# Tiles of 32 channels by 4 states in the scan stage of a graph kernel

## The chip, the cores and the metric

The kernel runs on one core of a Trainium2 chip. The metric is the time of the whole launch in microseconds of the device. Engines: PE is TensorE's matmuls, PEld its weight loads, DVE is VectorE, ACT is ScalarE, POOL is GpSimd, SP issues most of the DMAs. Each engine takes its instructions in the order in which they are queued.

## The reference

Two layers, each a graph convolution and then a mixture of experts, on 4096 rows of 256. The change lies in the first convolution of the first layer, which ends in a state-space scan:

```python
h = relu(adj @ x @ gcn_w + gcn_b)             # then a layer norm over the 256 features
xz = h @ w_in                                 # 512 channels xc, 512 channels z
u = silu(causal_conv4(xc) + conv_b)
dbc = u @ w_xp                                # 16 for dt, 16 for B, 16 for C
dt = softplus(dbc[:, :16] @ w_dt + b_dt)
dA  = exp(dt[:, :, None] * A[None])           # A = -exp(A_log), 512 channels x 16 states
dBu = dt[:, :, None] * B[:, None, :] * u[:, :, None]
def step(hst, inp):                           # over the 4096 rows
    dAt, dBut, Ct = inp
    hst = dAt * hst + dBut
    return (hst, hst @ Ct)                    # sum over the 16 states
y = (ys + u * D_skip) * silu(z);  x = x + y @ w_out
```

Everything is float32. The second half of the layers (routing, experts, top-k graph) is outside the change.

## The kernel before, in words

The scan stage goes over 8 chunks of 512 rows (`CW`), each in 32 steps (`STEPS`). Channels lie on partitions, 128 to a block (4 blocks, `MB`), rows along the free dimension. One step handles one channel block and two of the 16 states: 128 x 2 x 512 elements, in order of halves (two blocks), pairs of states (`g`), block in the half (`mi`).

- `inputs` (L1353): for each pair of states SP loads two rows of B (`bb`) and of C (`cb`) onto all partitions, 512 KB each. POOL multiplies `du = dt*u` with `bb` into `db` (L1363, two buffers).
- `decay` (L1368): ACT computes exp(dt*A) of one state into a bank of PSUM (`da`, three banks in turn).
- `scan` (L1384): one DVE scan per state over 512 rows, in place in `db`, starting from `state`.
- `product` (L1391): ACT copies the last column to `state`; DVE multiplies `db` with `cb` into `hc` (L1396, six buffers).
- `pair` (L1398): a DMA of POOL's queue adds the second half of `hc` onto the first.
- `total` (L1404): PE adds `hc` into `psy` with a 128 x 128 identity, one matmul of 512 columns a step; the first adds `u * D_skip` with a diagonal matrix. In the last chunk, from step 8 on, two matmuls take the place of the pair DMA.
- `gate` (L1418): DVE multiplies a finished block of `psy` with silu(z), a step after its last total.

Beside the scan of chunk c runs the front of chunk c+1, and the graph product of chunk c+2. The order of PE, DVE, ACT and POOL is written out by hand: `Front.PLAN` and `Front.EARLY` list by step what the front does (steps from 32 on fall into the chunk's own scan), in the loop at L1512. EARLY pieces stand between the scans and the product, PLAN pieces after the totals. `propagation` (L854) is the graph product: 64 pieces of two matmuls a chunk with tiles `at` of the adjacency matrix, 512 KB each, three buffers, four pieces to a tile. A planner (L1430 to 1441) puts the pieces into steps by costs of PE and DVE (`PE_STEP`, `DVE_STEP`, `PE_COST`, `DVE_COST`). SP's DMAs are queued by the framework's scheduler. `dt` and `du` of a whole chunk (`abs`, `exp`, `plus`, `log` on ACT, four `soft` operations on DVE, each for both halves) are finished before the chunk's first step, in SBUF. A total for step n-4 is emitted at step n. `Tail` and `Norm` blocks (output product, next norm) run in the last two chunks; `Last` closes the stage.

## Time and profile before

| | us |
|---|---|
| median of 3 runs | 2307.77 (2306.41 to 2309.53) |
| the profiled execution, its time | 2304.35 |
| its span, first to last instruction | 2302.6 |
| first scan to last scan of the stage | 159.4 to 1248 |
| a steady chunk of 32 steps | 136.5 |
| granted TensorE clock, mean | 0.951 |

The lines shown from here on are of this one execution. A line of the timeline gives the start, the time from the first start to the last end, engine, line, operation, tile written and tiles read, shape, count, and in brackets how long the engine had been idle and for what. A matmul in float32 shows as two passes, each with a weight load; its ends are modelled, so a busy PE may still have room. "issue" is idle time for which the profile shows no cause.

### The profile page before, as it was taken

What the parts mean: (1) busy time and instruction counts of PE and PEld (TensorE: products, weight loads), DVE (VectorE), ACT (ScalarE), POOL (GpSimd) and SP (SyncE); (2) the same over time, 40 slices, a digit from 0 to 9 for tenths busy, and PEclk for the clock granted to TensorE, in tenths of its full rate; (3) what the DMA queues carried; (4) which work ended last, traced back from release to release, by engine and by line L of the source; (5) the groups of instructions that cost most, each with busy time, mean ns of one, the idle gap of its engine ahead of it and who ended that gap; (6) DMA issues with size and microseconds to landing.
All of it is one profiled execution on the core that took longest, in us unless ns stands there. A gap on an engine that the chain in (4) does not pass through costs nothing. (4 is left out here: it accounts for less than half of the span.)

```text
span 2302.6 us, 28211 instructions
## 1 busy us (share of the span) xinstructions
PE 2103.2 (91%) x8291; PEld 1504.2 (65%) x8291; DVE 1801.3 (78%) x3193; ACT 1211.5 (53%) x2080; POOL 1395.4 (61%) x1057
## 2 busy tenths in 40 slices
PE   7899999999999999999799699996899989899994
PEld 6665565666646566555466588784588778678773
DVE  6949999999999999999998889314448999954342
ACT  4145746566575556657675232322488778533221
POOL 1028778777877877687764444442067777856652
PEclk9999999999999999999899799998899999999997
DMA  8549999998999999899885899863365555477794
GB/s 293 174 143 261 235 271 251 255 265 220 280 245 272 245 242 281 217 288 269 232 280 171 279 325 357 255 214 122 105 195 178 176 164 174 138 232 221 250 316 154
DMA packets 302678, 532.30 MB, mean 231 GB/s; under 512 B 31323, under 2 KB 170575, under 8 KB 301616
## 3 DMA queue, kind: packets, MB, share of 16 engines
q1 hardware_dynamic: 244720, 416.84, 55.7%
q0 software_dynamic: 57792, 113.54, 22.1%
q8 instruction: 69, 1.13, 0.2%
q14 instruction: 97, 0.79, 0.1%
HBM read 434.34 MB, written 49.02 MB: 210 GB/s over the span
## 5 line engine op out<-in xcount | busy, mean ns | idle before, releaser
L1363 POOL TENSOR_TENSOR db<-du,bb 128x1024 f32<-128x1024 f32 x256 | 607.7, 2374 | 322.0 <-ACT state L1392 72.0
L1386 DVE TENSOR_TENSOR_SCAN db<-da,state,db 128x512 f32<-128x512 f32 x512 | 627.3, 1266 | 23.9 <-ACT da L1379 21.4
L871 PE MATMUL pt<-at,gn 128*128 128x256 f32 x2048 | 487.4, 392 | 30.6 <-ACT pts L877 15.2
L871 PEld LDWEIGHTS pt<-at,gn 128*128 128x128 f32 x2048 | 401.7, 197 | 151.5 <-issue 63.2
L1379 ACT ACTIVATE da<-dt,negA 128x512 f32<-128x512 f32 x512 | 345.5, 688 | 236.4 <-DVE db L1386 226.3
L1396 DVE TENSOR_TENSOR hc<-db,cb 128x1024 f32<-128x1024 f32 x256 | 328.3, 1283 | 17.8 <-issue 0.4
L1875 PE MATMUL pf<-gn,f 128*128 128x256 f32 x1280 | 290.8, 388 | 0.0
L1413 PE MATMUL psy<-hc,ident 128*128 128x512 f32 x560 | 287.2, 606 | 0.0
L1875 PEld LDWEIGHTS pf<-gn,f 128*128 128x128 f32 x1280 | 248.3, 195 | 37.6 <-issue 3.3
L712 PE MATMUL ps_h<-xkT,wk 128*128 128x256 f32 x864 | 214.1, 390 | 13.3 <-DVE xkT L737 9.7
L697 PE MATMUL ps_y<-wk,hk 128*128 128x256 f32 x864 | 214.5, 383 | 0.2
L702 DVE TENSOR_TENSOR yk<-ps_y,bk 128x512 f32<-128x512 f32 x73 | 50.2, 687 | 204.6 <-PE ps_y L697 187.6
L1400 POOL DMA_DIRECT2D hc<-hc x232 | 202.5, 873 | 0.2
L712 PEld LDWEIGHTS ps_h<-xkT,wk 128*128 128x128 f32 x864 | 159.8, 194 | 49.3 <-DVE xkT L737 14.9
L1737 POOL DMA_INDIRECT x<-gnd,ls_idx x128 | 149.6, 1169 | 59.5 <-DMA gnd<-gn 20.1
L697 PEld LDWEIGHTS ps_y<-wk,hk 128*128 128x128 f32 x864 | 161.8, 192 | 21.7 <-ACT hk L716 1.4
L1413 PEld LDWEIGHTS psy<-hc,ident 128*128 128x128 f32 x560 | 105.5, 195 | 79.5 <-issue 56.5
L1737 POOL DMA_INDIRECT ring<-gnd,ls_idx x88 | 109.5, 1245 | 31.3 <-DVE x L1753 11.8
L1006 PE MATMUL ps_xz<-hT,w_in 128*128 128x512 f32 x256 | 116.5, 598 | 5.6 <-ACT zs L1019 4.1
L716 ACT ACTIVATE hk<-ps_h,d0r_b 128x256 f32<-128x256 f32 x104 | 48.9, 473 | 136.1 <-PE ps_h L712 136.1
L1023 PE MATMUL ps_xz<-xc,dK 128*128 128x512 f32 x256 | 114.8, 592 | 0.0
L1857 ACT ACTIVATE f<-at 128x1024 f32<-128x1024 f32 x80 | 84.4, 1055 | 50.1 <-PE pf L1875 41.1
(403 smaller groups left out, 3024.2 us busy)
## 6 DMA issues: line engine op xcount, KB each, us to landing
at<-in_adjT_dram SPq DMA_DIRECT2D x208, 512.0 KB, 5.0
bb<-bcd SPq DMA_DIRECT2D x128, 512.0 KB, 5.4
cb<-bcd SPq DMA_DIRECT2D x128, 512.0 KB, 5.2
hc<-hc POOLq DMA_DIRECT2D x232, 256.0 KB, 4.7
wk<-in_L_ffn_W_dram SPq DMA_DIRECT2D x70, 512.0 KB, 6.2
wk<-in_L_ffn_expert_w_dram SPq DMA_DIRECT2D x114, 256.0 KB, 4.2
ls_at<-in_adj_dram SPq DMA_DIRECT2D x32, 512.0 KB, 8.5
hc<-in_adj_dram SPq DMA_DIRECT2D x16, 512.0 KB, 4.7
```

The costliest lines, as they stand in the source:

```text
L697: nc.tensor.matmul(ps[:, j, :], hT[:, m, j * P:(j + 1) * P], w[:, m, :], start=(m == 0), stop=(m == kb_out - 1),)
L712: nc.tensor.matmul(ps[:, j, :], w[:, d, m * P:(m + 1) * P], xT[:, d, :], start=(d == 0), stop=(d == DB - 1),)
L871: nc.tensor.matmul(pt[:, k, :], xl[:, j, k * P:(k + 1) * P], at[:, jj, :], start=(j == 0 and k == 0), stop=(j == NT - 1 and k == DB - 1),)
L1006: nc.tensor.matmul(ps, w_in[:, k, m * P:(m + 1) * P], self.hT[:, k, :], start=(k == 0), stop=(k == DB - 1),)
L1363: nc.gpsimd.tensor_tensor(self.db, self.f.du[self.half][:, self.mi:self.mi + 1, :].to_broadcast([P, 2, CW]), self.bb, ALU.mult,)
L1379: nc.scalar.activation(da, self.f.dt[self.half][:, self.mi, :], AF.Exp, scale=negA[:, self.m, n:n + 1])
L1386: nc.vector.tensor_tensor_scan(self.db[:, j, :], da, self.db[:, j, :], state[:, self.m, n:n + 1], ALU.mult, ALU.add,)
L1396: nc.vector.tensor_tensor(self.hc, self.db, self.cb, ALU.mult)
L1400: nc.gpsimd.dma_start(self.hc[:, 0, :], self.hc[:, 1, :], accum_op=ALU.add)
L1413: nc.tensor.matmul(f.psy[m], ident, self.hc[:, j, :], start=False, stop=(self.g == GS - 1 and j == last),)
L1737: nc.gpsimd.indirect_dma_start(out=to[:, :], out_offset=None, in_=gnd[:, :], in_offset=bass.IndirectOffsetOnAxis(ap=lists.idx[:, q, s:s + ...
L1875: nc.tensor.matmul(pf[:, t, :], f[:, jj, t * P:(t + 1) * P], gn[:, j, :], start=(j == 0 and t % 2 == 0), stop=(j == NT - 1 and t % 2 == 1),)
```

## The change

A tile now holds 32 channels by 4 groups of states on its 128 partitions: partition 32r + k is channel k of the 32, with states 4r to 4r+3. A step takes 32 channels (`q`, four to a block) and two of the four states of each group (`p`, `j`), still 128 x 2 x 512 elements and 32 steps a chunk.

- `dt` and `du` are written to DRAM by halves of the channels (`dtd`, 1 MB) and read back spread over the four groups (`spread`, `dtu`, 512 KB, five buffers, emitted five steps ahead). B and C come four times a chunk (`states`). `soft` work is split by halves of the channels; the second half of it runs in steps 29 to 32.
- One scan goes over both halves of a step, 1024 elements. The first decay of the second half stays 0, so that the scan starts anew there; what is carried from the chunk before is added to that element beforehand by ACT (`join`, with exp(dt*A) of the first row from `carried`). Two `da` tiles of two banks each take the place of three banks; decays are emitted two steps ahead.
- The product with C stands one step behind the scan, `db` has three buffers, and `inputs` of step n+2 follow the product of step n-1.
- `total` takes two steps at a time, at least six steps back (`LAG`): for each half of the rows and each of the two steps, one matmul with `pick` (128 x 32, sums the four groups) writes the 32 partitions of `psy` that belong to `q`. `psy` has one buffer.
- The plan, the fill before the first step, the start of the front (`BEGIN`) and the closing of the stage move accordingly; `dp.place` and the last norm use `da`'s banks.

```diff
-        ps_y = s1.enter_context(tc.tile_pool(name="ps_y", bufs=2, space=PSUM, reuse_waits="tile"))
+        ps_y = s1.enter_context(tc.tile_pool(name="ps_y", bufs=1, space=PSUM, reuse_waits="tile"))
...
-        STEPS = H * 2 * GS
+        G4 = P // 32
+        STEPS = MB * G4 * (NS // 4) // 2
+        BEGIN = 3
+        LAG = 6
-        FILL = {11: 8, 12: 2, 14: 1, 17: 3, 19: 1, 22: 3, 23: 1, 24: 2, 25: 3, 26: 40}
...
-        PIECE, PE_STEP, DVE_STEP = 1.0, 1.1, 4.3
...
+        FILL = {6: 8, 7: 2, 9: 1, 12: 3, 14: 1, 17: 3, 18: 1, 19: 2, 20: 3, 21: 40}
+        FILLED = {7: 1, 8: 2}
+        PIECE, PE_STEP, DVE_STEP = 1.0, (1.8, 0.1), 4.25
+        PE_COST = {"gcn": 2.5, "turn": 0.8, "xz": 2, "conv": 4, "project": 2, "dt": 1}
+        DVE_COST = {"stats": 1.4, "soft": 1.45}
-        banks = ["d0", "d1", "d2"]
+        da = [ps_a.tile([P, 2, CW], F32, name=f"da{k}", tag=f"d{k}") for k in range(2)]
...
+                3: ["gcn 0", "gcn 1"], 4: ["biased 0", "biased 1"], 6: ["normal"],
+                7: ["fill 7", "turn 0", "turn 1"],
+                8: ["turned 0", "turned 1", "fill 8", "xz 0", "xz 1"], 9: ["in 0", "in 1"],
+                10: ["conv 0"], 11: ["conv 1"], 12: ["silu 0"], 13: ["xz 2", "xz 3"],
+                14: ["in 2", "in 3"], 15: ["conv 2"], 16: ["conv 3"], 17: ["silu 1"],
+                18: ["project 0", "project 1"], 19: ["scatter", "dt 0", "dt 1"],
+                20: ["abs 0", "abs 1", "exp 0"], 21: ["plus 0"], 22: ["log 0"],
+                25: ["dt 2", "dt 3"], 27: ["abs 2", "abs 3", "exp 1"], 28: ["plus 1"],
+                29: ["log 1"],
+                37: ["xz 4", "xz 5"], 38: ["in 4", "in 5", "xz 6", "xz 7"],
+                39: ["in 6", "in 7"], 44: ["silu 2"],
...
+                5: ["stats 0", "stats 1", "root"],
+                22: ["soft 0 0"], 23: ["soft 0 1"], 24: ["soft 0 2"], 25: ["soft 0 3"],
+                29: ["soft 1 0"], 30: ["soft 1 1"], 31: ["soft 1 2"], 32: ["soft 1 3"],
...
+                self.dtd, self.dtu, self.bc = {}, {}, {}
...
             def do_abs(self, m):
                 ps = self.ps.pop(("dt", m))
+                b = m % H
+                if b == 0:
+                    self.sp = w1p.tile([P, H, 2, CW], F32, name="sp", tag="tmp")
+                    self.t1 = w1p.tile([P, H, CW], F32, name="t1", tag="h")
+                    self.dt, self.du = self.sp[:, :, 0, :], self.sp[:, :, 1, :]
+                nc.scalar.activation(self.du[:, b, :], ps, AF.Abs, bias=b_dt[:, m:m + 1])
+                nc.scalar.activation(self.dt[:, b, :], ps, AF.Relu, bias=b_dt[:, m:m + 1])
+            def do_exp(self, a):
+                nc.scalar.activation(self.du, self.du, AF.Exp, scale=-1.0)
+            def do_plus(self, a):
+                nc.scalar.activation(self.t1, self.du, AF.Identity, bias=1.0)
+                nc.scalar.activation(self.t1, self.t1, AF.Identity, bias=minus1[:, :1])
+            def do_log(self, a):
+                nc.scalar.activation(self.du, self.du, AF.Ln, bias=1.0)
+            def do_soft(self, a, i):
+                t1, dt, du = self.t1, self.dt, self.du
...
+                    nc.vector.tensor_tensor(
+                        du, dt, self.us[:, a * H:a * H + H, :], ALU.mult
+                    )
+                    self.dtd[a] = dram.tile([P, H, 2, CW], F32, name=f"dtd{self.c}_{a}")
+                    nc.sync.dma_start(self.dtd[a], self.sp)
+                    fronts[self.c] = self
+            def spread(self, g):
+                m, q = divmod(g, G4)
                 a, b = divmod(m, H)
...
+                rows = self.dtd[a][32 * q:32 * q + 32, b]
+                t = self.dtu[g] = w2p.tile([P, 2, CW], F32, name="dtu", bufs=5)
+                nc.sync.dma_start(
+                    t, bass.AP(rows.tensor, rows.offset, [(0, G4)] + list(rows.ap))
+                )
+            def states(self, k, p):
+                r0 = NS * (k == "c") + 2 * p
+                rows = self.bcd[r0:r0 + 2, :]
+                t = self.bc[k, p] = w2p.tile([P, 2, CW], F32, name=f"{k}b{p}", bufs=1)
+                nc.sync.dma_start(
+                    t, bass.AP(rows.tensor, rows.offset,
+                               [(NS // G4 * CW, G4), (0, 32)] + list(rows.ap))
+                )
...
-                self.db = w2p.tile([P, 2, CW], F32, name="db")
+            def __init__(self, n):
+                self.n = n
+                self.c, self.i = divmod(n, STEPS)
+                self.m, r = divmod(self.i, 2 * G4)
+                self.p, self.q = divmod(r, G4)
+                self.g = G4 * self.m + self.q
+                self.f = fronts[self.c]
+                self.dtu = self.f.dtu[self.g]
+                self.paired = self.c < NC - 1 or self.i < 8
+            def inputs(self):
+                self.db = w2p.tile([P, 2, CW], F32, name="db", bufs=3)
                 nc.gpsimd.tensor_tensor(
...
+                    self.db, self.dtu[:, 1:2, :].to_broadcast([P, 2, CW]),
+                    self.f.bc["b", self.p], ALU.mult,
+                )
+            def carried(self):
+                return e0[:, self.m % 2, self.q, :]
+            def decays(self):
+                m, q, p = self.m, self.q, self.p
+                if self.c > 0 and p == 0:
+                    nc.scalar.activation(
+                        self.carried(), negA[:, q, m, 1::2], AF.Exp, scale=self.dtu[:, 0, 0:1]
+                    )
+                for j in range(2):
+                    s_ = 2 * p + j
+                    nc.scalar.activation(
+                        da[self.n % 2][:, j, j:], self.dtu[:, 0, j:], AF.Exp,
+                        scale=negA[:, q, m, s_:s_ + 1],
+                    )
+            def join(self):
+                if self.c > 0:
+                    first = self.db[:, 1, 0:1]
+                    nc.scalar.activation(
+                        first, state[:, self.g, 2 * self.p + 1:2 * self.p + 2], AF.Identity,
+                        scale=self.carried()[:, self.p:self.p + 1], bias=first,
+                    )
+            def scan(self):
+                flat = self.db.rearrange("p a t -> p (a t)")
                 nc.vector.tensor_tensor_scan(
...
+                    flat, da[self.n % 2].rearrange("p a t -> p (a t)"), flat,
+                    state[:, self.g, 2 * self.p:2 * self.p + 1], ALU.mult, ALU.add,
+                )
+            def keep(self):
+                if self.c < NC - 1:
+                    nc.scalar.copy(
+                        state[:, self.g, 2 * self.p:2 * self.p + 2], self.db[:, :, CW - 1]
+                    )
             def product(self):
...
                 self.hc = w2p.tile([P, 2, CW], F32, name="hc", bufs=6)
...
+                nc.vector.tensor_tensor(self.hc, self.db, self.f.bc["c", self.p], ALU.mult)
...
+            def total(self, other):
                 f, m = self.f, self.m
...
+                if self.p == 0 and self.q == 0:
+                    f.psy = ps_y.tile([P, CW], F32, name="psy", tag="psy")
+                    nc.tensor.matmul(f.psy, dD[:, m, :], f.us[:, m, :], start=True, stop=False)
                 last = 0 if self.paired else 1
                 for j in range(last + 1):
...
+                    for w in range(2):
+                        for st in (self, other):
+                            r, t = slice(32 * st.q, 32 * st.q + 32), slice(w * HW, w * HW + HW)
+                            nc.tensor.matmul(
+                                f.psy[r, t], pick, st.hc[:, j, t], start=False,
+                                stop=(self.p == 1 and j == last and w == 1),
+                            )
+                return self.p == 1 and other.q == G4 - 1
             def gate(self):
...
+                u = self.f.us[:, self.m, :]
+                nc.vector.tensor_tensor(u, self.f.psy, self.f.zs[:, self.m, :], ALU.mult)
...
-            negA = load(wp, a["L0_gnn_A_log"], "negA")
+            negA = wp.tile([P, G4, MB, NS // G4], F32, name="negA")
+            for r in range(G4):
+                for q in range(G4):
+                    nc.sync.dma_start(
+                        negA[32 * r:32 * r + 32, q],
+                        a["L0_gnn_A_log"][32 * q:32 * q + 32, :, 4 * r:4 * r + 4],
+                    )
...
-            state = wp.tile([P, MB, NS], F32, name="state")
+            state = wp.tile([P, MB * G4, NS // G4], F32, name="state")
+            e0 = wp.tile([P, 2, G4, 2], F32, name="e0")
+            pick = wp.tile([P, 32], F32, name="pick")
+            for r in range(G4):
+                sq = slice(32 * r, 32 * r + 32)
+                nc.scalar.copy(pick[sq, :], ident[sq, sq])
+            for k in range(2):
+                nc.vector.memset(da[k][:, 1, 0:1], 0.0)
...
-            for i in range(9, STEPS):
+            for i in range(4, 27):
...
+                if i == 6:
+                if i == 19:
+                    for p in range(2):
+                        fr.states("b", p)
+                        fr.states("c", p)
+                if i == 25:
+                    for g in range(G4):
+                        fr.spread(g)
...
+            ALL = NC * STEPS
+            for n in range(2):
+                steps.append(Step(n))
+                steps[n].inputs()
+                steps[n].decays()
+            fr = None
+            for n in range(ALL):
...
+                cur = steps[n]
+                if i == 6 and c > 0:
...
+                live = [(fronts[c], STEPS + i)] if n > 0 else []
+                if c == 0 and i < 6:
+                    live.insert(0, (fronts[0], 27 + i))
+                if i >= BEGIN and fr is not None:
+                    live.append((fr, i))
+                if n + 5 < ALL:
+                    c5, i5 = divmod(n + 5, STEPS)
+                    if i5 % (2 * G4) < G4:
+                        fronts[c5].spread(i5 // (2 * G4) * G4 + i5 % G4)
+                if fr is not None:
+                    if i == 27:
+                        fr.states("b", 0)
+                    elif i == 29:
+                        fr.states("c", 0)
+                    elif i == 30:
+                        fr.states("b", 1)
+                if i == 1 and c > 0:
+                    fronts[c].states("c", 1)
+                cur.scan()
+                cur.keep()
+                if n + 1 < ALL:
+                    steps[n + 1].join()
+                if n + 2 < ALL:
+                    steps.append(Step(n + 2))
+                    steps[n + 2].decays()
+                for f, k in live:
+                    f.at(k, Front.EARLY)
...
+                if n > 0:
+                    steps[n - 1].product()
+                if n + 2 < ALL:
+                    steps[n + 2].inputs()
                 if n > 0:
                     steps[n - 1].pair()
...
+                for st in gated:
+                    st.gate()
                 gated = []
...
+                if summed <= n - LAG or (summed <= n - 3 and not steps[summed].paired):
+                    if steps[summed].total(steps[summed + 1]):
+                        gated.append(steps[summed])
+                    summed += 2
+                for f, k in live:
+                    f.at(k)
...
+            steps[-1].product()
+            last.first(1)
+            for m in range(H, MB - 1):
+                last.add(1, m)
+            last.residual(1)
+            while summed < ALL:
+                for st in gated:
+                    st.gate()
+                gated = []
+                if steps[summed].total(steps[summed + 1]):
+                    gated.append(steps[summed])
+                summed += 2
+            for st in gated:
+                st.gate()
+            for hh in range(2):
+                last.add(hh, MB - 1)
```

## The prediction

> **What bounds the kernel now.** I read the engine totals, the busy times by stage, and then the timeline of the scan stage engine by engine. First the totals and one steady stretch (columns: stretch, length, then busy time and count of PE, PEld, DVE, ACT, POOL, the granted clock, DMA share, GB/s):
>
> ```profile
> PE 2103.2 (91%) x8291; PEld 1504.2 (65%) x8291; DVE 1801.3 (78%) x3193; ACT 1211.5 (53%) x2080; POOL 1395.4 (61%) x1057
> ...
> 560.00:700.00 140.00, 136.79 (x458) 86.26 (x457) 134.11 (x122) 84.57 (x147) 104.54 (x66) 0.98 0.94 255
> ```
>
> Both PE and DVE are nearly full there. The chunks' first scans start at 159.4, 294.7, 431.3, 567.8, 704.3, 840.9, 977.4 and 1117.3 us: a steady chunk of 32 steps takes 136.5 us. The timeline tells which engine paces one plain step:
>
> ```profile
> 703.19 1.23 DVE L1396 TENSOR_TENSOR hc<-db,cb 128x1024 f32<-128x1024 f32 x1
> ...
> 704.33 2.45 DVE L1386 TENSOR_TENSOR_SCAN db<-da,state,db 128x512 f32<-128x512 f32 x2
> ...
> 704.58 2.34 POOL L1363 TENSOR_TENSOR db<-du,bb 128x1024 f32<-128x1024 f32 x1 [0.81 <-DVE hc L1396]
> ...
> 706.87 0.88 POOL L1400 DMA_DIRECT2D hc<-hc  x1
> ...
> 706.88 1.22 DVE L1396 TENSOR_TENSOR hc<-db,cb 128x1024 f32<-128x1024 f32 x1
> ...
> 708.02 2.45 DVE L1386 TENSOR_TENSOR_SCAN db<-da,state,db 128x512 f32<-128x512 f32 x2
> ```
>
> 704.33 to 708.02 is 3.69 us, and DVE has no idle in it: DVE paces. Two scans take 2.45; the product starts 0.10 after they end (it reads their result), 0.17 more than the 1.19 from one scan to the next; the next scan starts 1.14 after the product. POOL starts 0.16 after a product ends (it refills a buffer that the product read) and ends at 706.92, just as the next product begins. What happens when these two meet:
>
> ```profile
> 603.92 2.35 POOL L1363 TENSOR_TENSOR db<-du,bb 128x1024 f32<-128x1024 f32 x1 [2.14 <-ACT state L1392]
> ...
> 605.75 1.59 DVE L1396 TENSOR_TENSOR hc<-db,cb 128x1024 f32<-128x1024 f32 x1
> ...
> 614.08 2.34 POOL L1363 TENSOR_TENSOR db<-du,bb 128x1024 f32<-128x1024 f32 x1
> ...
> 615.66 1.84 DVE L1396 TENSOR_TENSOR hc<-db,cb 128x1024 f32<-128x1024 f32 x1
> ```
>
> The product ends 1.07 and 1.08 after POOL's multiply (607.34 against 606.27, 617.50 against 616.42), however early it started: the two exclude each other. The scans beside POOL's multiply keep their 1.26. So POOL's 2.35 must fit under the scans, and now it just does.
>
> ACT is in order, and a long block on it delays the decays:
>
> ```profile
> 597.42 1.28 ACT L1030 ACT_TABLE_LOAD   x1
> 598.71 1.92 ACT L1030 ACTIVATE zs<-zs 128x2048 f32<-128x2048 f32 x1
> 600.53 0.57 ACT L877 COPY pts<-pt 128x512 f32<-128x512 f32 x1
> 601.12 1.28 ACT L1379 ACT_TABLE_LOAD   x1
> ```
>
> and on DVE:
>
> ```profile
> 603.20 2.46 DVE L1386 TENSOR_TENSOR_SCAN db<-da,state,db 128x512 f32<-128x512 f32 x2 [1.08 <-ACT da L1379]
> ```
>
> A 5.05 us block costs 1.08: about 4.0 us of ACT work after a step is free today. On PE, a change of array shape shows:
>
> ```profile
> 602.01 0.69 PE L946 MATMUL ps_gcn<-gcn_b,onesf 1*128 1x256 f32 x2
> 602.64 1.13 PE L941 MATMUL ps_gcn<-gcn_w,pts 128*128 128x256 f32 x4
> 603.70 0.69 PE L946 MATMUL ps_gcn<-gcn_b,onesf 1*128 1x256 f32 x2
> ```
>
> Passes of 256 columns run 0.213 us apart in long rows (20 in 4.48), so two take 0.43 and four 0.85; here 0.63 and 1.06, so 0.2 per change of shape. Into and out of the 48-column matmul of `project` it is 0.10 (663.73 to 664.68, where two passes of 512 need 0.85) and 0.16 (664.68 to 668.25, where eight need 3.41).
>
> **The change part by part.**
>
> *DVE, scan.* The trace has no scan of 1024. Rows of 54, 264 and 512 elements (250, 704 and 1262 ns) lie on 2.2 ns an element and 0.13 us fixed: 2.39. The ends are 2.32 (the slope of 2.125 between the rows of 136 and 264) and 2.45 (what two take, nothing saved); I take 2.39, the line through three rows. Its neighbours overlap it by 0.07 as they do now. The product, a step behind, no longer waits for its scan: 0.17 goes. DVE alone would need 2.39 − 0.07 + 1.14 = 3.46.
>
> *POOL under it.* `inputs` of step n+2 refills the buffer that the product of step n−1 reads (three buffers), so POOL still starts 0.155 after a product, works 2.345, and the next product ends 1.08 later: 0.155 + 2.345 + 1.08 = 3.58. That is the new plain step: the saving is 0.11, not 0.23. POOL's queue (2.35 + 0.87 for the pair DMA) fits into 3.58. The ends are 3.46, if POOL does not hold the product, and 3.69, if nothing is won.
>
> *Other DVE work of a chunk.* Eight soft pieces of 1.14 as before (spread one to a step), statistics 2.4, four gates (now 0.57; behind a gate POOL has time, so 0.45 over the 3.58). 32 × 3.58 + 8 × 1.14 + 2.4 + 1.8 = 127.9, against 136.5 now, of which some 4.4 are waits for ACT.
>
> *ACT.* Added per step: `join`, one element per partition, like the 0.19 copy of `state` (0.10 from start to next start); half a `carried`, 0.05. The cost is in the order. The next scan waits for `join(n+2)`, which stands behind `keep(n+1)` and all plan work of step n. After a scan's end ACT does keep, join, two decays (0.63 each), 1.75 with the wait for POOL; keep and join of the next step want 0.4; the second scan on would start 2 × 3.58 − 2.33 = 4.83 after. Free ACT work: 4.83 − 2.15 = 2.7, against 4.0 now. The blocks, from the rows: `silu 2` and `silu 0` in one step, 1.28 + 1.82 + 1.2 + 1.28 = 5.58: waits 2.4 behind a gate of 0.45. `silu 1` 3.76 and about 0.4 for PE: 1.5. `abs`,`abs`,`exp` 4 × 0.57 + 0.95 = 3.25, twice: 0.6 together. Normalizing and the `in` copies: 0.7. Together 5.2, ends 2 (the blocks overlap with late POOL) and 9 (each copy also finds PE late). The two added loads of the log's table (2.56) fall into soft steps, 1.14 longer; the shared silu load gives as much back.
>
> *PE.* Per pair of steps, two passes of 512 twice (4 × 0.427 = 1.71) become eight of 256 columns with 32 outputs. One after the other, 8 × 0.213 = 1.71, plus shape changes like `project`'s 0.26: 1.97. All overlapped two by two: 0.85 + 0.26 = 1.11. No row shows passes in different columns at once; I take 1.5, the middle. A chunk's passes (152 × 0.427 + 280 × 0.213 + 0.9) and shape changes (2.6) are 128 us; 16 × (1.5 − 1.71) makes it 125, ends 118 and 132. The "TensorE: Matmul & The Clock Gate" page of the Trainium skill (Part 3) says that matmuls on distinct column groups run at once in order, 2.38 times the rate with three groups. By it, with the two passes of one product following each other in the same group, five slots of 0.213 and the changes are, as an estimate by that page, 1.33, so 122 us a chunk; no row here shows it, and the sum stays. "TensorEngine Tiling (Array Packing)", Key Properties, speaks against: each change of tiling mode drains the array; the rows of 0.2 and 0.16 agree. Slack shrinks: a product's buffer waits for the totals emitted one step earlier (two now), so PE may lag 2 us, not 6. I charge 1.0 a chunk, between 0 and 5.
>
> *DMA.* 32 loads of 512 KB for `bb`/`cb` go; 4 + 16 come, and two stores of 1 MB: bytes fall. Hidden, but on SP's queue the first `dtu` load waits for the store, and adjacency tiles stand behind it. The 1 MB store of `yd` lands in 8.9; three tiles in hand keep PE busy for 3 × 3.4 and some 2.6 of other work, 12.8, and the next lands 8.9 + 5.7 after: about 2 us of PE, in its slack and in the 1.0.
>
> *Start.* Now soft work ends at 157.2 and the scan starts at 159.4. After: dt 0/1 at 132, then 10 pieces of 0.86 to the copy of `pts` at 141.6 that ACT waits for, log to 143.9, three soft pieces to 147.4, store 8.9 or less for an otherwise free queue (7), load 5, POOL 2.4: 162.1, so +2.7 (ends 0 and 8). Chunk 0 gets three soft pieces more: 114.6 + 12.5 + 2.4 + 1.4 + 5.2 = 136.1 against 135.3: +0.8. 16 small `negA` loads lie under list building.
>
> *Last chunks and end.* Chunk 6 (139.9 now) keeps its tails, with tighter ACT: −0.5. Chunk 7: −3.5 − 0.5 for steps and gates, +1.1 soft, +3 for Norm blocks: 0. After the last scan one block of `add` instead of two (−1.7), a pair of totals more: −0.5.
>
> **Sum.** Steady chunk 127.9 + 5.2 + 1.0 = 134.1, so −2.4; five of them −12.0; −0.5 − 0.5 + 0.8 + 2.7: −9.5. The profiled execution took 2304.35 (span 2302.6); it becomes 2294.9. The median of the runs is 3.4 higher: 2298.
>
> **The rivals.**
> *Waits vanish*: ACT and PE waits 2 a chunk, since the decays are two steps ahead. For: two buffers of two banks. Against: `join` is not ahead. 5 × (6.6) + 4 for chunk 6 − 3: 34 less, 2274.
> *PE becomes the bound* (the other side): passes in different columns don't overlap, 132 a chunk, and PE's waits for ACT's copies (2.6 and 0.6 in the chunk from 567.8) and for tiles (2) no longer fit into the slack: 137. It decides from 136.0, where the start's loss is not earned back. 6 × 0.5 + 3.5: 2314. For: PE's 136.8 of 140. Against: those 140 hold stretched passes.
> *ACT's chain binds*: waits 9 and PE 1.0: 137.9 a chunk, 5 × 1.4 + 5: 2320; for, 4.0 falls to 2.7; against, blocks are spread.
> *It doesn't do what it says*: the freed DVE time is only POOL's turn, 3.69 stays: 134.1 + 3.5 = 137.6 a chunk, 6 × 1.1 + 3.5: 2318. For: POOL already ends as the product starts. Against: the 1.07 and 1.08.
>
> **How the numbers follow.** Forecast 0.45 (own range 2288 to 2308, ACT's waits from 3.5 to 7), waits vanish 0.20, PE 0.17, ACT 0.10, no gain 0.08. The range takes in 2274 with 6 below it (a wait of 1 less a chunk) and 2320 with 4 above (the start's end of 8). A change of 0.2% (4.6 us) is about what a measurement of this kernel can tell from none. Faster, below 2303.2: 0.32 of the forecast's 0.45 and the 0.20. Within: 0.13 of the forecast and 0.06 of PE's. Slower: the rest, 0.29.
>
> **What would show it.** Right: scans of 1024 at 2.39; plain steps 3.58 apart with POOL 0.15 behind each product; products of 1.35 instead of 1.23; DVE idle behind `join`, most at step 12; first scan near 162. Wrong: steps at 3.46; DVE waiting for PE at `hc` or `psy`; pick passes 0.213 apart in one row (serial), or PE waiting for `at`.

## The result: 2738.5 us, 18.7% slower

The changed kernel takes 2738.5 us (2734.3 to 2740.8), the kernel before 2307.1 beside it; the ratio is 1.1867, with a 95% interval of 1.1846 to 1.1888. The forecast was 2298 us, with a range of 2268 to 2324. The profiled execution has a span of 2738.8 us. By the first scans of the chunks, with the kernel before in brackets: the scan starts at 197.0 us (159.4), chunk 0 takes 192.6 (135.3), a steady chunk 187.7 (136.5), chunk 6 165.3 (139.9), chunk 7 up to its last step 187.8 (129.6), and what follows 1057.4 (1055.7). So 38 of the 436 us lie ahead of the first scan, 397 between the first scan and the last step, 256 of these in the five steady chunks, and under 2 behind.

The totals of the page and one steady chunk of the changed kernel (columns as in the first fence of the prediction):

```profile
PE 2126.7 (78%) x8851; PEld 1486.3 (54%) x8851; DVE 1787.8 (65%) x2939; ACT 1309.3 (48%) x2390; POOL 1402.6 (51%) x1057
...
765.10:953.00 187.90, 135.03 (x506) 79.97 (x505) 128.39 (x87) 97.94 (x194) 104.09 (x65) 0.85 0.61 162
```

DVE works 128.4 us in the chunk, as forecast (127.9 and some overlap); the other 59 it waits. The waits of that chunk (engine, line, what ended the wait, then the sum, the number and the longest):

```profile
DVE hc L1422 <- PE psy L1440: 66.2, 6, 25.9
...
PE pt L873 <- DMA at<-in_adjT_dram: 43.7, 5, 21.6
ACT e L1388 <- DMA dtu<-dtd: 22.3, 7, 4.2
...
DVE db L1409 <- ACT db L1402: 16.0, 8, 4.8
```

DVE waits for totals, PE for adjacency tiles, ACT for `dtu`: at the root stand DMAs. The DMA share is 0.61 where it was 0.94, and the bytes of the run fell (498.76 MB against 532.30), so it is not the bandwidth as a whole. The granted clock is 0.85 in the chunk (0.98 before); the stretches below in which PE does nothing have 0.50, so the lower clock goes with the waits. The longest step of the chunk, 30 us, on PE:

```profile
946.47 2.07 PE L873 MATMUL pt<-at,gn 128*128 128x256 f32 x4 [21.63 <-DMA at<-in_adjT_dram]
...
950.17 1.67 PE L1440 MATMUL psy<-hc,pick 128*32 128x256 f32 x8
```

and on DVE, whose product needs the buffer that these totals read:

```profile
951.88 1.23 DVE L1422 TENSOR_TENSOR hc<-db,cb 128x1024 f32<-128x1024 f32 x1 [25.88 <-PE psy L1440]
```

SP's queue in the same stretch shows why the tile is late (start, time until the last issue is done, count):

```profile
904.91 9.43 SPq L1110 DMA_DIRECT2D dtu<-dtd  x3
914.44 7.42 SPq L1119 DMA_DIRECT2D cb<-bcd  x1
921.96 6.16 SPq L795 DMA_DIRECT2D at<-in_adjT_dram  x1
928.21 7.32 SPq L1110 DMA_DIRECT2D dtu<-dtd  x1
935.62 4.75 SPq L795 DMA_DIRECT2D at<-in_adjT_dram  x1
```

A single issue takes 4.75 to 7.42 us. In the five steady chunks of the kernel before, no issue of this queue takes over 1 us:

```profile
858.21 0.32 SPq L1359 DMA_DIRECT2D bb<-bcd  x1
858.58 0.43 SPq L795 DMA_DIRECT2D at<-in_adjT_dram  x1
```

What the DMA engines do meanwhile, in stretches in which only one kind of load is in flight. The changed kernel, with `dtu` and `bb` loads alone (the two numbers at the end are the share of the 16 DMA engines and GB/s):

```profile
936.00:941.00 5.00, 0.00 (x0) 0.00 (x0) 0.00 (x0) 0.00 (x0) 0.00 (x0) 0.50 0.26 104
946.00:948.00 2.00, 1.53 (x4) 1.26 (x5) 0.00 (x0) 0.00 (x0) 0.00 (x0) 0.50 0.25 104
```

The kernel before, with `bb` or `cb` loads of the same 512 KB alone:

```profile
844.80:846.40 1.60, 1.60 (x8) 1.21 (x7) 1.60 (x2) 0.54 (x1) 1.60 (x1) 1.00 1.04 412
852.00:853.80 1.80, 1.80 (x7) 1.14 (x6) 1.80 (x2) 0.57 (x1) 1.66 (x1) 1.00 0.83 335
```

A load of the changed kernel keeps a quarter of the DMA engines busy and moves 104 GB/s; one of the kernel before kept 0.83 of them or all busy and moved 335 to 412. A packet of 4 KB takes 0.159 us (median) in both kernels: the engines in use are not slower, there are fewer of them. In the changed kernel the access pattern of `dtu`, `bb` and `cb` begins with the four groups of states (`[(0, G4)]` in `spread`, `[(NS // G4 * CW, G4), (0, 32)]` in `states`); in the kernel before it begins with 128 partitions. The Trainium skill has the rule in "DMA: Bandwidth & Descriptors", section "Why a DMA increments its semaphore by 16 and not by 1": the number of engines is the largest up to 16 that divides the outermost size of both sides, and a DMA from SP takes the lowest-numbered ones. The shares of 0.25 and 0.26 agree with the first half; no row names an engine, so the second is not shown here.

That the loads share their four engines with the tiles is shown by the tile for which PE waits until 946.47. The DMA records of the trace have its 512 packets of 1 KB from 941.04 to 945.65. The first three quarters of them are done by about 943.4, at a DMA share of 0.91; the last 126 run beside 4 KB packets of the loads, and together these keep a quarter of the engines busy:

```profile
943.40:946.00 2.60, 0.00 (x0) 0.00 (x0) 0.00 (x0) 0.00 (x0) 0.00 (x0) 0.50 0.28 91
```

That gives **theory A**: the 20 loads of a chunk all go through the same four DMA engines. At 0.159 us a packet each of the four has 20 x 128 x 0.159 / 4 = 102 us of loads, and its share of what runs on all: tiles 24, pair DMAs 47, stores 7.5. Together that is an estimate of 180 us, worked out from the packet times of the trace, in a chunk that takes 187.7. **Theory B** is the one place where the prediction saw a danger: SP's queue is in order, and stores and reloads that wait for the scan hold the tiles behind them.

### The profile page after: what moved, and what is told of

The parts are those of the page before. It is cut to its first block, busy times and chain, and to the rows that moved or that the text cites. A ratio compares the mean times of both kernels' runs of the same rounds, so it can differ in the third digit from the quotient of the medians.

```text
span 2738.8 us, 28761 instructions
## 1 busy us (share of the span) xinstructions
PE 2126.7 (78%) x8851; PEld 1486.3 (54%) x8851; DVE 1787.8 (65%) x2939; ACT 1309.3 (48%) x2390; POOL 1402.6 (51%) x1057
## 2 busy tenths in 40 slices
DMA packets 291397, 498.76 MB, mean 182 GB/s; under 512 B 30283, under 2 KB 169535, under 8 KB 288288
## 3 DMA queue, kind: packets, MB, share of 16 engines
q0 software_dynamic: 57792, 113.54, 18.6%
## 5 line engine op out<-in xcount | busy, mean ns | idle before, releaser
L1377 POOL TENSOR_TENSOR db<-dtu,bb 128x1024 f32<-128x1024 f32 x256 | 613.9, 2398 | 736.8 <-DVE hc L1422 407.6
L873 PE MATMUL pt<-at,gn 128*128 128x256 f32 x2048 | 535.0, 417 | 308.9 <-DMA at<-in_adjT_dram 299.0
L1409 DVE TENSOR_TENSOR_SCAN db<-da,state,db 128x1024 f32<-128x1024 f32 x256 | 599.7, 2342 | 197.2 <-ACT db L1402 147.0
L873 PEld LDWEIGHTS pt<-at,gn 128*128 128x128 f32 x2048 | 416.4, 209 | 439.7 <-DMA at<-in_adjT_dram 284.3
L1422 DVE TENSOR_TENSOR hc<-db,cb 128x1024 f32<-128x1024 f32 x256 | 337.5, 1319 | 267.2 <-PE psy L1440 263.6
L1393 ACT ACTIVATE da<-dtu,negA 128x512 f32<-128x512 f32 (+1 forms) x512 | 350.2, 684 | 70.6 <-DMA dtu<-dtd 58.5
L1416 ACT COPY state<-db 128x2 f32<-128x2 f32 x224 | 42.6, 190 | 297.2 <-DVE db L1409 297.2
L1440 PE MATMUL psy<-hc,pick 128*32 128x256 f32 x1120 | 169.2, 431 | 1.9 <-DMA hc<-hc 1.9
L1012 PE MATMUL ps_xz<-hT,w_in 128*128 128x512 f32 x256 | 133.8, 671 | 29.5 <-ACT hT L996 16.9
L1440 PEld LDWEIGHTS psy<-hc,pick 128*32 128x32 f32 x1120 | 59.6, 119 | 115.0 <-issue 85.6
```

What stands on the lines that cost most here:

```text
L873: nc.tensor.matmul(pt[:, k, :], xl[:, j, k * P:(k + 1) * P], at[:, jj, :], start=(j == 0 and k == 0), stop=(j == NT - 1 and k == DB - 1),)
L1012: nc.tensor.matmul(ps, w_in[:, k, m * P:(m + 1) * P], self.hT[:, k, :], start=(k == 0), stop=(k == DB - 1),)
L1377: nc.gpsimd.tensor_tensor(self.db, self.dtu[:, 1:2, :].to_broadcast([P, 2, CW]), self.f.bc["b", self.p], ALU.mult,)
L1393: nc.scalar.activation(da[self.n % 2][:, j, j:], self.dtu[:, 0, j:], AF.Exp, scale=negA[:, q, m, s_:s_ + 1],)
L1409: nc.vector.tensor_tensor_scan(flat, da[self.n % 2].rearrange("p a t -> p (a t)"), flat, state[:, self.g, 2 * self.p:2 * self.p + 1], ALU. ...
L1422: nc.vector.tensor_tensor(self.hc, self.db, self.f.bc["c", self.p], ALU.mult)
```

## The experiments

Kernels that stand in one group ran on the same chip, beside the kernel before. Its time was 2308.5, 2372.9, 2309.4, 2310.7 and 2309.2 us in the five groups; differences are to that. In the second group (e5 to e8) both kernels were slower: the part behind the scan stage takes 1123 to 1131 us in its traces, at a granted clock of 0.90 to 0.91 where the trace of the kernel before has 0.93. Chunk times and first scans come from the traces and are compared with the trace of the kernel before. A row without a ratio rests on one execution.

### Which loads, and is it the shape

*e1* cuts every load into four of 32 partitions, *e2* only `dtu`, *e3* only `bb` and `cb`:

```diff
-                nc.sync.dma_start(
-                    t, bass.AP(rows.tensor, rows.offset, [(0, G4)] + list(rows.ap))
-                )
+                for r in range(G4):
+                    nc.sync.dma_start(t[32 * r:32 * r + 32], rows)
...
+                for r in range(G4):
+                    rows = self.bcd[r0 + NS // G4 * r:r0 + NS // G4 * r + 2, :]
+                    nc.sync.dma_start(t[32 * r:32 * r + 32], rows.partition_broadcast(32))
```

*e4* is the kernel before, with only the shape of its `cb` loads changed (C is stored four times, by four stores of 32 KB a chunk, so that the pattern can begin with four):

```diff
-                        nc.sync.dma_start(t, self.f.bcd[r0:r0 + 2, :].partition_broadcast(P))
+                    rows = self.f.cd4[0, r0:r0 + 2, :]
+                    nc.sync.dma_start(
+                        self.cb, bass.AP(rows.tensor, rows.offset,
+                                         [(NS * CW, 4), (0, 32)] + list(rows.ap))
+                    )
```

> Every load of dtu, bb and cb is cut into four loads of 32 partitions each (outermost count 32 in place of 4); order on SP's queue, bytes and everything else as in the changed kernel. Theory A (a load whose outermost count is 4 runs on four of the 16 DMA engines): in the changed kernel each of those four has, per steady chunk, 20 loads x 128 packets x 0.159 us / 4 = 102 us, adjacency tiles 16 x 512 x 0.046 / 16 = 24, pair DMAs 32 x 128 x 0.184 / 16 = 47, stores 3 x 128 x 0.314 / 16 = 7.5, together 180 us, near the chunk of 187.7; cut up, it is 104 us an engine, so the chunk falls to what DVE needs, 134 to 139 us, the run to 2295 to 2335 us, and no issue on SP's queue takes over 1 us. Theory B (SP's queue holds the adjacency tiles behind loads and stores that wait for others): the order is the same, so the chunk stays above 175 us and the run above 2650 us.

> Only the 16 dtu loads of a chunk are cut into 32 partitions each; bb and cb keep an outermost count of 4. Theory A: each of the four engines has 4 x 128 x 0.159 / 4 = 20 us of bb and cb, 20 of dtu, 78 of the rest, 119 us: below DVE's 134, so the chunk is 134 to 141 us and the run 2295 to 2350 us. Theory B: above 2650 us.

> Only the four bb and cb loads of a chunk are cut into 32 partitions each; dtu keeps an outermost count of 4. Theory A: each of the four engines has 81 us of dtu, 5 of bb and cb, 78 of the rest, 165 us in place of 180, so the chunk is 165 to 175 us and the run 2580 to 2660 us. Theory B: what holds SP's queue are above all the stores and the reloads of bb and cb, which wait as before: 2700 to 2740 us.

> The kernel before, where C is stored four times in DRAM and each cb load reads its 128 partitions as 4 x 32 rows (outermost count 4): the same 512 KB, the same place on SP's queue, two buffers as before. Theory A: each of the four engines has, per chunk, 16 x 128 x 0.159 / 4 = 81 us of cb, 20 of bb, 24 of tiles, 47 of pair DMAs, 2.5 of the yd store, 175 us in place of the 136.5 of a chunk: the run takes 2550 to 2640 us. Theory B: no wait is added, the run stays at 2300 to 2330 us.

| | time | against before | first scan | steady chunk |
|---|---|---|---|---|
| e1, all cut | 2438.2 | ratio 1.0556 (1.0534 to 1.0579) | 176.7 | 147 to 153 |
| e2, `dtu` cut | 2611.3 | +302.8 | 196.2 | 171 to 175 |
| e3, `bb`, `cb` cut | 2667.2 | +358.7 | 176.3 | 177 to 181 |
| e4, before with `cb` by four | 2680.9 | +372.4 | 159.7 | 179 to 186 |

e4 settles the mechanism: one access pattern, with the same bytes at the same place in the queue, takes the kernel *before* from 136.5 to about 181 us a chunk (175 expected by theory A, 136.5 by B; the run is above A's 2550 to 2640). Where its trace has 4 KB packets alone (of `cb` and `bb`), it shows the quarter again:

```profile
443.60:446.80 3.20, 0.33 (x1) 0.30 (x2) 2.72 (x3) 2.40 (x6) 1.64 (x1) 1.00 0.25 104
```

e1 returns 300 of the 436 us with the order of the queue as it was. But the sums of A are only a floor: all four chunk times lie above them. e2 was to come down to 134 to 141 us a chunk and stayed at 171 to 175: four loads by four engines, 20 us of work, still cost most of it. They stand in one stretch of steps (27 to 33), in front of the tiles; that this bunching is the reason is argued, not tested. In e2 the issue that follows the tiles behind `cb` is held, and PE, which waits for them, starts 14 us after the first of them was issued:

```profile
679.96 0.54 SPq L1118 DMA_DIRECT2D cb<-bcd  x1
680.80 1.12 SPq L795 DMA_DIRECT2D at<-in_adjT_dram  x2
682.05 8.43 SPq L1111 DMA_DIRECT2D dtu<-dtd  x4
...
694.83 6.31 PE L873 MATMUL pt<-at,gn 128*128 128x256 f32 x20 [25.58 <-DMA at<-in_adjT_dram]
```

This fits the tile seen above, which is spread over all engines and complete with the slowest four. e3, too, is above its 165 to 175. And e1, which was to reach 134 to 139, left some 14 us a chunk in two places, the steps at i = 3 and i = 31 (10.3 to 12.9 us each); 20 of its 500 issues in the five chunks still take over 1 us, at most 2.1.

### The same loads uncut, and the queue

*e5* lets partition 4k + r hold channel k and group r (`pick` and the 16 small `negA` loads are changed to match), so that each load is one DMA again, whose pattern begins with 32:

```diff
-                    t, bass.AP(rows.tensor, rows.offset, [(0, G4)] + list(rows.ap))
+                    t, bass.AP(rows.tensor, rows.offset, ap[:1] + [(0, G4)] + ap[1:])
...
-                               [(NS // G4 * CW, G4), (0, 32)] + list(rows.ap))
+                               [(0, 32), (NS // G4 * CW, G4)] + list(rows.ap))
...
+            nc.vector.tensor_reduce(
+                pick, ident.rearrange("p (k r) -> p k r", r=G4), AX.X, ALU.add
+            )
```

*e6* is e5 with the `dtd` stores on ACT's queue, *e7* with the loads of `bb` and `cb` there too; *e8* does what e7 does to the changed kernel with its loads as they are (`nc.sync.dma_start` becomes `nc.scalar.dma_start` in `do_soft` and `states`).

> The changed kernel with partition 4k + r in place of 32r + k for channel k and group r (in pick, in negA, in the loads): each load of dtu, bb and cb is again one DMA at its old place on SP's queue, with an outermost count of 32. In the run with the loads cut up, 15 us of a chunk of 149.7 are left in two places, the steps at i = 3 and i = 31. Theory B (SP's queue): the store dtd_1 waits for the last soft piece of step 32, the reloads of bb and cb for the last use in steps 27 to 31, with tiles of the adjacency matrix behind them; the order is the same, so both stalls stay at 5 to 8 us each, a chunk is 145 to 151 us and the run 2390 to 2440 us. Theory C (the stalls come from the 60 loads more that the cutting made): both go, a chunk is 134 to 138 us, the run 2300 to 2330 us.

> As e5_interleaved, and the two dtd stores of a chunk are issued on ACT's queue, right where the last soft piece stands. Theory B: the stall at i = 3 goes (SP no longer waits for the soft piece of step 32), that at i = 31 stays, since bb and cb are still reloaded on SP's queue: 5 to 8 us a chunk less than e5_interleaved, run 2340 to 2390 us. Theory C: no difference from e5_interleaved beyond 10 us.

> As e6_store_act, and the four loads of bb and cb are issued on ACT's queue too. Theory B: SP's queue holds nothing more that waits for the scan but dtu, both stalls go, a chunk is 133 to 138 us, the run 2290 to 2325 us. Theory C: no difference from e5_interleaved beyond 15 us, or slower by ACT's six issues a chunk (6 x 0.4 us).

> The changed kernel with its loads as they are (outermost count 4), and only the dtd stores and the loads of bb and cb moved to ACT's queue. Theory A (four of 16 DMA engines carry the loads, 180 us of work each in a chunk): no order of issues helps, a chunk stays at 170 to 190 us, the run at 2600 to 2750 us. Theory B alone: both stalls go and the run falls to 2300 to 2400 us.

| | time | against before | first scan | steady chunk |
|---|---|---|---|---|
| e5 | 2396.4 | +23.5 | 172.7 | 136.2 |
| e6, stores on ACT | 2415.0 | +42.1 | 171.0 | 136.2 |
| e7, stores, `bb`, `cb` on ACT | 2407.3 | ratio 1.0143 (1.0106 to 1.0180) | 171.8 | 135.9 |
| e8, changed kernel, on ACT | 2841.8 | +468.9 | 190.4 | 180 to 198 |

Theory B falls as a cause by itself. With the loads mended and SP's order untouched, the stall at i = 3 is gone (3.68 us, as a plain step) and the step at i = 31 is down to 5.4 to 6.0; the 14 us of e1 came from the 60 loads more. Relieving SP's queue then gives nothing in the steady chunks, and with the loads by four it gives nothing at all (e8; four of its five steady chunks, and its run, are above theory A's 170 to 190 and 2750). e6 is 18.6 us above e5, where at most 10 was expected; by the traces that lies in chunk 0, chunk 7 and behind the scan stage, not in the steady chunks. A stretch of e5 with 4 KB packets of the mended loads alone keeps all DMA engines busy and moves 402 GB/s:

```profile
530.90:532.00 1.10, 1.10 (x4) 0.32 (x3) 1.10 (x2) 1.02 (x3) 0.90 (x2) 1.00 1.02 402
```

Four consecutive chunks of e5, and what DVE waits for in them:

```profile
448.70:993.90 545.20, 502.80 (x2017) 303.34 (x2016) 517.51 (x346) 391.84 (x776) 413.04 (x260) 0.95 0.86 224
```

```profile
DVE hc L1423 <- PE psy L1441: 11.8, 16, 1.2
DVE db L1410 <- ACT db L1403: 8.5, 16, 0.7
DVE t L1091 <- ACT t L1083: 6.9, 8, 1.1
```

This is the kernel that the prediction spoke of: 136.2 us a chunk against the 134.1 forecast. It is still 23.5 us above the kernel before. Against the trace of the kernel before it loses 13.3 in the start, 4.8 in chunk 0 and 9.8 in chunk 7 up to its last step, and wins 1.5 in the steady chunks and 1.2 in chunk 6, 25.2 together; what follows can't be compared, since that trace is not of this group.

### The start, the lead of the totals, the join

*e9* is e5 with the 16 `negA` loads on ACT's queue; *e11* is e5 with `LAG = 4`; *e12* is e5 without `join` and `carried` (what is carried into the second half of each step is left out of the computation); *e10* is e9 with `LAG = 4` and the fill's 40 pieces behind step 26. With `LAG = 4` the first block of a chunk is multiplied with z before its silu, so e10 and e11 compute that block differently.

> As e5_interleaved, with the 16 small negA loads issued on ACT's queue in place of SP's. In e5_interleaved the first adjacency tile behind them is issued at 47.3 us (40.5 in the kernel before) and the first scan starts at 172.7 (159.4). Theory S (these loads hold the tiles and the rows for list building that stand behind them on SP's queue, and the whole start with them): the first scan comes 9 to 12 us earlier, at 161 to 164, the rest is as in e5_interleaved, so the run is 11 to 16 us over the kernel before. Rival (they lie under the list building, as forecast; the later start comes from the path through DRAM alone): first scan at 170 to 173 us, run 20 to 27 us over the kernel before.

> As e5_interleaved, with LAG 4 in place of 6, so that a product's buffer is given back by totals that stand two or three steps earlier in PE's order. In e5_interleaved DVE's products wait 2.9 us a chunk for totals, its scans 2.1 us for join. Theory P (the short lead of the totals makes these 2.9): chunk 133 to 134 us in place of 136.2, the run 14 to 21 us under e5_interleaved. Rival (PE then waits for the pair DMAs, which land 4.7 us after issue, two steps being 7.2): chunk 135.5 to 139 us.

> As e5_interleaved without join and carried: what is carried from the chunk before into the second half of each step is left out of the computation. In chunk 0, which has no join, plain steps are 3.58 us as forecast; in the later chunks they are 3.67, with POOL starting 0.24 instead of 0.15 after a product. Theory J (join makes POOL's next multiply wait for one engine more, 0.09 a step, and DVE's scans wait 2.1 a chunk): plain steps 3.58 in all chunks, a chunk 131 to 132.5 us. Rival (the 0.09 comes from something else that chunk 0 lacks): plain steps stay at 3.67, a chunk is 134 to 135.5.

> As e9_negA_act, with LAG 4, and with the 40 pieces of the graph product that stand before dt 2 and dt 3 of the first chunk moved behind step 26 of the fill. By theories S and P: first scan at 156 to 161 us (the copy of pts no longer stands before the log), no stall of 7 us in the third step of chunk 0, a chunk 133 to 134 us: the run 5 to 20 us under the kernel before (ratio 0.991 to 0.998). By the rivals: 15 to 25 us over it (ratio 1.006 to 1.011).

| | time | against before | first scan | steady chunk |
|---|---|---|---|---|
| e9 | 2338.4 | +29.0 | 175.6 | 135.9 |
| e11 | 2354.4 | +45.0 | 172.6 | 139.9 |
| e12 | 2308.7 | −0.7 | 172.1 | 133.1 |
| e10 | 2359.3 | ratio 1.0216 (1.0202 to 1.0230) | 169.5 | 139.8 |

e11 went to the rival: with the totals two steps earlier PE waits for the pair DMAs, the copy of `pts` on ACT waits for PE, and the scan for ACT (e11 over the same 545 us, which are 3.9 of its chunks):

```profile
PE psy L1441 <- DMA hc<-hc: 26.4, 11, 4.3
```

```profile
DVE db L1410 <- ACT db L1403: 25.3, 23, 2.3
```

e12 shows the price of `join` and `carried` together: plain steps are 3.57 to 3.58 in every chunk, and a chunk takes 133.1, or 3.1 us less (expected 131 to 132.5; DVE waits 3.9 for totals there). e9 did not tell its theories apart: on ACT's queue the loads stood behind the copy of `pts` and ran from 40.9 to 53.5 us, and DVE's sign change of `negA`, ahead of the list building, waited for them until 58; first scan and time lie above both of its ranges. e10 lies above both of its ranges too.

### Both mended

*e13* is e5 with `negA` from four loads of whole rows, and DVE operations that pick each partition's states, placed behind the first pieces of the second graph product:

```diff
+                nc.sync.dma_start(
+                    alog[:, q], bass.AP(rows.tensor, rows.offset, ap[:1] + [(0, G4)] + ap[1:])
+                )
...
+            nc.vector.tensor_scalar(to, frm[:, :, 0, :], own[:, 0:1], None, ALU.mult)
+            for r in range(1, G4):
+                nc.vector.scalar_tensor_tensor(
+                    to, frm[:, :, r, :], own[:, r:r + 1], to, ALU.mult, ALU.add
+                )
```

*e14*, *e15* and *e16* were meant to have two scans a step. As they ran, they kept the one scan of 1024, without `join`, `carried` and the restart between the halves, so that the state of the first half runs on into the second. Their expectations speak of two scans; what they tell is a chunk without `join` (e14), with the edit of e13 (e15), and with seven buffers of `hc` and four of `dtu` (e16). The routing behind the scan stage depends on the values: behind their last scan these three run 4417 passes on PE where e12 has 4273, and from their last step on they take 1099.6 to 1103.0 us where e12 has 1059.0, so their whole times can't be compared.

> As e5_interleaved, with negA made from four loads of whole rows of 64 (in place of 16 loads of 2 KB), and five small DVE operations that pick each partition's own four states, which stand behind the first 16 pieces of the second graph product instead of ahead of the list building. In e9_negA_act the loads left SP's queue but ran on ACT's from 40.9 to 53.5 us, and DVE's sign change of negA, ahead of the list building in DVE's queue, waited for them until 58, so that run did not tell the theories apart. Theory S (the 16 loads and the sign change behind them hold tiles and list building in the start): first scan at 161 to 165 us in place of 172.7, run 9 to 16 us over the kernel before. Rival: first scan at 169 to 173 us, run 20 to 27 us over it.

> As e5_interleaved, with two scans of 512 in each step again, each started from its own carried state, so that join and carried are not needed; all else stays, the product a step behind too. Theory J (join costs 3 us a chunk, and the plain step of 3.58 is set by POOL's hand-off 0.155 + 2.345 + 1.08, not by the scan: with two scans DVE alone needs 2.45 - 0.07 + 1.14 = 3.52): plain steps 3.57 to 3.60 in all chunks, a chunk 132.5 to 134 us, the run 6 us under to 6 over the kernel before. Rival (the one scan of 1024 earns the 0.11): plain steps 3.66 to 3.70, a chunk 136 to 138 us, the run 20 to 35 us over it.

> The edits of e13_negA_late and e14_two_scans together. By S and J: first scan 161 to 165, a chunk 132.5 to 134, the run 4 to 16 us under the kernel before (ratio 0.993 to 0.998). By the rivals: 20 us over it or more.

> As e15_both, with seven buffers for hc in place of six, and four for dtu in place of five to make room. Theory P' (DVE's products wait 3 to 4 us a chunk for totals that PE reaches late, and one buffer more covers it): a chunk 129.5 to 131.5 us, 12 to 25 us under e15_both. Rival (PE is later than one step where these waits fall, or dtu comes late with four buffers): a chunk within 1 us of e15_both or longer, the run within 7 us of it or above.

| | time | first scan | steady chunk |
|---|---|---|---|
| e13 | 2324.9 (+14.1) | 168.3 | 135.7 |
| e14 | 2346.6 | 172.3 | 133.1 |
| e15 | 2347.8 (ratio 1.0153, 1.0128 to 1.0177) | 169.9 | 133.0 |
| e16 | 2342.9 (ratio 1.0139, 1.0114 to 1.0164) | 169.2 | 133.3 |

The `negA` loads were a cause of the late start. They hold SP's queue, and the first adjacency tile behind them is issued at 47.2 us where it was 37.2 (the 40.5 in e9's expectation is the tile after it). The changed kernel:

```profile
39.88 5.09 SPq L1502 DMA_DIRECT2D negA<-in_L_gnn_A_log_dram  x8
...
47.22 0.38 SPq L795 DMA_DIRECT2D at<-in_adjT_dram  x1
```

In e5 PE then waits 10 us for that tile:

```profile
53.58 5.78 PE L873 MATMUL pt<-at,gn 128*128 128x256 f32 x16 [10.04 <-DMA at<-in_adjT_dram]
```

and the copy of `dbc` (ACT, L1050 before and L1056 after) comes at 141.64 us in place of 129.41. In e13 it comes at 134.90, so 6.7 of the 12.2 are back, though the first scan gains 4.4 only and misses its 161 to 165. Seven buffers of `hc`, with four of `dtu` (e16), do not shorten a chunk: the step at i = 31 falls from some 6.0 to 4.7 us, and those at i = 5 and i = 13 grow from 6.3 to some 7.9 and from 5.1 to 5.8.

*e17* has the two scans in truth, and the edit of e13 placed still later; *e18* also has the fill's 40 pieces behind step 26 (`26: 40` for `21: 40` in `FILL`).

```diff
-                nc.vector.tensor_tensor_scan(
-                    flat, da[self.n % 2].rearrange("p a t -> p (a t)"), flat,
-                    state[:, self.g, 2 * self.p:2 * self.p + 1], ALU.mult, ALU.add,
-                )
+                for j in range(2):
+                    s_ = 2 * self.p + j
+                    nc.vector.tensor_tensor_scan(
+                        self.db[:, j, :], da[self.n % 2][:, j, :], self.db[:, j, :],
+                        state[:, self.g, s_:s_ + 1], ALU.mult, ALU.add,
+                    )
...
-                if n + 1 < ALL:
-                    steps[n + 1].join()
```

> As e5_interleaved, with (1) two scans of 512 a step, each started from its own carried state, no join, no carried (in e14_two_scans, e15_both and e16_seven_hc the scan was still the one of 1024, without a restart between the halves, so they tell of a chunk without join, not of two scans); (2) negA made from four loads and five DVE operations that stand behind the list building's first part on SP's and DVE's queues. Theory J: plain steps 3.57 to 3.60 in every chunk although two scans take 2.45 in place of 2.34, a chunk 132.5 to 134 us. Theory S: dbc is copied at 129 to 131 us as in the kernel before (141.6 in e5_interleaved), first scan 160 to 164. Together: the last scan 11 to 17 us earlier than the kernel before's, the run 10 to 18 us under it, ratio 0.992 to 0.996. Rivals: the two scans cost 0.08 to 0.11 a step (3.66 to 3.69, chunk 136 to 137.5): ratio 1.001 to 1.005; first scan at 167 or later: 5 us more.

> As e17_two_scans_late, with the 40 pieces of the graph product behind step 26 of the fill in place of step 21, so that dt 2, dt 3 and the log of the first chunk don't stand behind them. ACT's log then waits no longer for the copy of pts (3.2 us), and the third step of chunk 0 no longer for dt (7 us); but the front of chunk 1 needs these pieces at step 3. If that is later than now: first scan 3 us earlier, chunk 0 up to 3 us longer, the run 0 to 3 us under e17_two_scans_late. If PE catches up by then: 5 to 9 us under it.

| | time | ratio | first scan | chunk 0 | steady chunk |
|---|---|---|---|---|---|
| e17 | 2302.5 | 0.9971 (0.9959 to 0.9983) | 167.1 | 140.3 | 133.1 |
| e18 | 2304.1 | 0.9976 (0.9964 to 0.9988) | 160.8 | 148.7 | 133.1 |

e17 is faster than both kernels, though only 0.3% faster than the kernel before. Its DVE, with two scans in 2.45 us, keeps the same 3.58 from step to step as the one scan of 2.34 in e12:

```profile
643.43 1.28 DVE L1420 TENSOR_TENSOR hc<-db,cb 128x1024 f32<-128x1024 f32 x1
644.64 2.45 DVE L1407 TENSOR_TENSOR_SCAN db<-da,state,db 128x512 f32<-128x512 f32 x2
647.01 1.28 DVE L1420 TENSOR_TENSOR hc<-db,cb 128x1024 f32<-128x1024 f32 x1
648.22 2.45 DVE L1407 TENSOR_TENSOR_SCAN db<-da,state,db 128x512 f32<-128x512 f32 x2
```

```profile
644.86 2.35 POOL L1378 TENSOR_TENSOR db<-dtu,bb 128x1024 f32<-128x1024 f32 x1 [0.41 <-ACT da L1390]
...
648.45 2.34 POOL L1378 TENSOR_TENSOR db<-dtu,bb 128x1024 f32<-128x1024 f32 x1 [0.42 <-DVE hc L1420]
```

A product ends at 644.71, POOL starts 0.15 later, works 2.35, and the next product ends 1.08 after it, at 648.29. So the fused scan earns nothing here, and what it needs, `join` and `carried`, costs 3.1 us a chunk. What a plain step gains, 3.58 for 3.69, is then left to the product a step behind, which no longer waits for its own scan; no run tests that alone. e18 moved the wait and did not remove it: the first scan is 6.3 us earlier, chunk 0 is 8.4 longer, with 14.4 us in its fourth step, where ACT's copy of `pts` waits 10.0 for the moved pieces. e17 missed its start (160 to 164), and with it its 10 to 18 us: 6.8. Its copy of `dbc` comes at 132.65, 9.0 of the 12.2 us earlier, but the first scan only 5.6: the path from that copy to the first scan has grown to 34.5 us (30.0 before). In e18 it is 28.7, so the 40 pieces on PE stand in that path.

## Why the prediction was wrong, step by step

**The DMA step failed**, and with it the time. The prediction counted bytes ("bytes fall"), called the 20 loads "hidden", and priced the one danger on SP's queue at "about 2 us of PE". It took for the new loads, without saying so, that 512 KB move as the `bb` rows of the trace did. It did not read the access patterns in the diff: a pattern that begins with four keeps a quarter of the DMA engines busy for 5 us, where the old one kept most or all of them busy for 1.3 to 1.6. Those four engines then had an estimated 180 us of work in a chunk, the tiles and the pair DMAs with them. e4 shows that this alone is enough (136.5 to 181), and e5 that mending it alone brings the chunk from 187.7 to 136.2. The wait was named right ("PE waiting for `at`" among the signs of a wrong forecast), its cause was not; as e5 to e8 show, the order of SP's queue was not it. None of the four rivals held it, and the range of 56 us had no term for it. Nor would the forecast have held with the loads mended: e5 is 23.5 us slower than the kernel before, where 9.5 faster was forecast, by the start, the totals' lead, `join` and chunk 7 below.

The other steps, read from the changed kernel and, where its stalls hide them, from e5:

- *The scan of 1024.* 2.34 us; forecast 2.39, ends 2.32 and 2.45. Right.
- *The plain step of 3.58.* Right in chunk 0 of e5 and in all chunks of e12 and e17, wrong by 0.09 (3.67) where `join` stands: POOL starts 0.24 after a product in place of 0.15. Why the join delays POOL was not found. The forecast said that the hand-off to POOL, not the scan, sets the step; e12 and e17, with scans of 2.34 and 2.45 and the same 3.58, show it.
- *ACT's waits, 5.2 a chunk (2 to 9).* In e5 the scan waits 2.1 for `join`, and the soft pieces 1.7 for ACT; 3.8 together. The forecast was on the high side, within its ends; by its own working it is 5.7, since two blocks of 3.25 over 2.7 make 1.1 and not 0.6.
- *PE.* A pair of totals was put at 1.5 (1.11 to 1.97; 1.33 as the estimate by the Trainium skill's "TensorE: Matmul & The Clock Gate", Part 3). It takes 0.98: in the changed kernel from 905.18 to 906.16:

```profile
905.18 1.06 PE L1440 MATMUL psy<-hc,pick 128*32 128x256 f32 x8
906.16 4.58 PE L873 MATMUL pt<-at,gn 128*128 128x256 f32 x20
```

  Four times 0.213 and 0.13 for the changes of shape; the two steps' column groups run fully beside each other, which is better than the estimate made by that page and than the low end. The rival "PE becomes the bound" is refuted: PE is busy 125.7 us a chunk in e5.
- *The totals' lead*, charged 1.0 a chunk (0 to 5): 2.95 in e5. A shorter lag makes the chunk longer (e11), one buffer more of `hc` with one less of `dtu` does not help (e16).
- *The chunk*: 134.1 forecast, 136.2 in e5: +2.0 for the lead, −1.4 for ACT, and the rest (1.5) about what 0.09 a step is worth.
- *The start*, +2.7 (0 to 8): +13.3 in e5. "16 small `negA` loads lie under list building" failed: they stand in front of the next tiles on SP's queue, 0.64 us an issue. Up to `dbc` the front is 12.2 us late; with `negA` loaded in four pieces 6.7 (e13) and 9.0 (e17) of these are back, and where the rest lies was not found. The path from `dbc` to the first scan, which the +2.7 was made for, grew by 1.1 in e5 (31.1 against 30.0), and by 4.5 in e17, where `dbc` is early. In the changed kernel the first scan is another 24 us later, by the `bb` and `cb` loads through four engines: with these cut it starts at 176.3 (e3), with `dtu` cut at 196.2 (e2).
- *Chunk 0, 6 and 7.* +0.8, −0.5 and 0 forecast; in e5 +4.8, −1.2 and, up to the last step, +9.8. In chunk 0 DVE waits 5.8 us at one step for the soft chain on ACT, which itself waits 3.2 for `dt 2`, behind 40 pieces of the graph product on PE; the forecast did not look there. In chunk 7 DVE waits 8.9 us for `join` and 3.0 for a Norm block.

With the loads mended, these misses make up e5's 23.5 us against the forecast −9.5, as far as the two groups can be compared.

## What to carry to other kernels

Read the access pattern of every new or moved DMA before its bytes: here an outermost size of four meant a quarter of the DMA engines, 32 or 128 most or all of them. Price a load by the engines that it gets, and add what else runs on those, since a tile that spans all sixteen was complete only with the slowest. A load that repeats rows over partition groups could here be given a long outermost dimension by interleaving the groups over the partitions. And before a scan or any other operation is fused, find what sets the step: here a hand-off between two engines did, and the fusion only bought a correction term.
